# Layers 1 to 3 of a four-layer convolution kernel: sums, quantisation and layer 1 at other places in a round, zeros by VectorE

## The chip, the cores and the metric

The kernel runs on one core of one Trainium2 chip. The metric is device time in microseconds, lower is better. A core has five engines that each work through a queue of their own in order: TensorE (matmuls, PE), VectorE (DVE), ScalarE (ACT), GpSimd (POOL) and SyncE (SP). DMA transfers are issued here from the queues of GpSimd and SyncE.

## The reference, cut to what matters

Four convolution layers follow each other on 32 images of 8 channels and 256 x 256 pixels. Each layer normalises its input by groups of two channels and adds its output to its input.

```python
# layer 0: 15 steps of a coupled map, a small network and a gate
x = x + L0(_gn(x), ...)

# layer 1: 3x3 convolution, 8 channels to 8, on quantised values
sx = 127 / max|x|;  sw = 127 / max|weight|
qx = clip(round(x * sx), -127, 127);  qw = clip(round(weight * sw), -127, 127)
x = x + (conv(qx, qw) / (sx * sw) + bias)          # x inside is _gn(x)

# layer 2: 3x3 convolution, 8 channels to 8
x = x + (conv(_gn(x), weight) + bias)

# layer 3: 5x5 mean filter on each channel
x = x + depthwise_conv(_gn(x), weight)

def _gn(v, G=4, eps=1e-5):      # mean and variance over two channels and all pixels of an image
    return (v - mean) / sqrt(var + eps)
```

The maximum of |x| in layer 1 runs over all 32 images, so layer 1 cannot begin before layer 0 has finished with the last one.

## The kernel before, in words

Layer 0 fills the first five sixths of the span and is not touched. What follows is the second block of the kernel, which does layers 1, 2 and 3 for all images.

**Tiles.** For layers 1 and 2 an image lies in 128 partitions, 16 row classes times 8 channels, with 16 image rows of each class behind one another in a partition, 4096 values in all. The input of layer 1 is `qh` (bf16), that of layer 2 `xh` (fp32); both have one column of zeros at each side of a row. A convolution of a chunk of 512 outputs (`conv3`) is three matmuls on `qh` or `xh`, one for each horizontal shift, and a fourth on `qb` or `xb2`: 48 of their 72 rows hold the neighbour rows that lie in another partition. `beside` fills them with two DMAs of 24 rows from `qh` or `xh` on SP's queue. An image has 8 chunks (`NCH`). An fp32 matmul takes two passes of 0.43 us of TensorE, a bf16 matmul one of about 0.22. For layer 3 the partitions are 128 image rows, the tile `xr` has two halves (k) and 8 channels, and `xr2` holds the rows beyond the halves, filled by `beside3`.

**A round.** The loop over b runs through 35 rounds. In round b layer 3 works on image b-3, layer 2 on image b-1 and layer 1 on image b. A round has two halves, each run by `among(work, tasks)`: it takes up to eight steps of the generator `work` and after step i runs the tasks listed for i. The order in which these calls are made is the order in each engine's queue (`manual_schedule`); no scheduler reorders it.

- First half: the work is `layer3`, two steps for each group of two channels. After the first step (four matmuls of half 0), the second step has the four matmuls of half 1, the four halo and end matmuls, and two additions by VectorE (L831). The tasks are the sums of layers 1 and 2 of the last round, the normalisation of layer 2's input (`normal2`, L760) with the DMAs for `xb2`, the four quantisations of layer 1's input (`quantize1`: three VectorE operations of 1024 columns, L741, L703, L704, and one on ScalarE, L705) with the DMAs for `qb`, and `by_group`.
- Second half: the work is `both`, which alternates a chunk of layer 2 and a chunk of layer 1. The tasks are the four normalisations of layer 3's input (`normal3`, L792) and `beside3`. Layer 2 ends with 16 stores to DRAM on GpSimd's queue (L776), from where `load3` reads the image back as `y` in the layout of layer 3. Behind it GpSimd loads `x1`, the input of layer 1, a round ahead.

**Sums.** `stats_parts` is a generator in five parts: two `bn_aggr` at the round's end (L101, by `begin`), then a matmul over partitions and four small VectorE operations (L104 to L108), another matmul and an addition (L111, L112), a root on ScalarE (L115), and five small VectorE operations (L117 to L121). `by_group` turns layer 2's sums into scalars for layer 3: two VectorE operations (L131), a matmul (L133) and a copy (L135), all in one call.

**Order before.** In the first half, after step i: part i of both sums for i from 0 to 3, the one of layer 2 first; `normal2` after step 3; quantisation k after step k; `qb`'s DMAs after step 4; `by_group` after step 5. In the second half chunk i of layer 2 is followed by chunk i of layer 1. PSUM for the chunks is a pool of five buffers (`psv`), that for the sums one of three.

**Before the first round** the six tiles `qh`, `qb`, `xh`, `xb2`, `xr` and `xr2` are set to zero by GpSimd (L719), the scales of the quantisation are computed (`top`, L150 to L162, and L697 to L700), and the weights of layer 1 are quantised.

Of the kernel before, what the change touches and what calls it, by code (L numbers as in the profile page):

```python
# [22 lines left out]
HP, WP = H + 2, W + 2  # L23
# [37 lines left out]
def window(ap, offset, dims):  # L61

    return bass.AP(ap.tensor, ap.offset + offset, [list(d) for d in dims])
# [3 lines left out]
def kernel(  # L67
# [3 lines left out]
    nc = tc.nc  # L71
    B = x.shape[0]
# [54 lines left out]
    def by_group(psum, st):  # L127

        sel = small.tile([P, 4, 2], F32, name="sel")
        for j in range(2):  # L130
            nc.vector.tensor_scalar(sel[:, :, j], gsel_sb, st[:, j : j + 1], None, ALU.mult)  # L131
        ps = psum.tile([P, 512], F32, name="ps")
        nc.tensor.matmul(ps[:, 0:8], ones, sel.rearrange("p a b -> p (a b)"), start=True, stop=True)  # L133
        got = small.tile([P, 4, 2], F32, name="got")
        nc.vector.tensor_copy(got.rearrange("p a b -> p (a b)"), ps[:, 0:8])  # L135
        return got

    def beside(queue, t, src, q):


        row, long = HB * WP, (HB - 1) * WP - 2
        for i, (p, to, at) in enumerate(((P - C, 1, 0), (0, 0, 1))):
            queue.dma_start(
                t[q + 24 * i : q + 24 * i + 24, :, :].rearrange("p k w -> p (k w)")[
                    :, to * WP : to * WP + long
                ],
                window(src, p * row + at * WP, [[row, C], [1, 3], [1, long]]),
            )
# [19 lines left out]
    with ExitStack() as es:  # L168
# [6 lines left out]
        psum = es.enter_context(tc.tile_pool(name="ps_a", bufs=3, space=PSUM))  # L175
# [503 lines left out]
    with ExitStack() as es:  # L679
        wt = es.enter_context(tc.tile_pool(name="wt1", bufs=1))  # L680
        two = es.enter_context(tc.tile_pool(name="two", bufs=2))
        psum = es.enter_context(tc.tile_pool(name="ps_b", bufs=3, space=PSUM))
# [19 lines left out]
        def quantize(dst, t, s):  # L702
            nc.vector.tensor_scalar(t, t, s, MAX_Q, ALU.mult, ALU.min)  # L703
            nc.vector.tensor_scalar(t, t, -MAX_Q, ROUND, ALU.max, ALU.add)  # L704
            nc.scalar.activation(dst, t, AF.Copy, bias=-ROUND)  # L705
# [5 lines left out]
        qh = wt.tile([P, HB, WP], BF16, name="qh")  # L711
        qb = wt.tile([72, HB, WP], BF16, name="qb")
        xh = wt.tile([P, HB, WP], F32, name="xh")
        xb2 = wt.tile([72, HB, WP], F32, name="xb2")

        xr = wt.tile([P, 2, C, W + 4], F32, name="xr")
        xr2 = wt.tile([72, C, W + 4], F32, name="xr2")
        for t in (qh, qb, xh, xb2, xr, xr2):
            nc.gpsimd.memset(t, 0.0)  # L719

        def conv3(src, near, w, i):
            ps = ps_v.tile([P, 512], F32, name="psv")
            o = ps.rearrange("p (k w) -> p k w", w=W)
            for dx in range(3):
                nc.tensor.matmul(  # L725
                    o, w[:, dx, :], src[:, 2 * i : 2 * i + 2, dx : dx + W],
                    start=dx == 0, stop=False,
                )
            nc.tensor.matmul(  # L729
                o, w[0:72, 3, :], near[:, 2 * i : 2 * i + 2, 0:W], start=False, stop=True  # L730
            )
            return ps

        def load1(b):
            x1 = two.tile([P, NPX], F32, name="x1")
            nc.gpsimd.dma_start(x1, x1_d[b])
            return x1

        def quantize1(b, x1, k):
            t = two.tile([P, 1024], F32, name="tq")  # L740
            nc.vector.tensor_scalar(  # L741
                t, x1[:, bass.ts(k, 1024)], stat1[:, b, 0:1], stat1[:, b, 1:2],
                ALU.subtract, ALU.mult,
            )
            quantize(
                qh[:, 4 * k : 4 * k + 4, 1 : 1 + W],
                t.rearrange("p (r w) -> p r w", w=W), sc[:, 0:1],
            )

        def layer1(b, x1, x2, bn):  # L750
            for i in range(NCH):
                ps = conv3(qh, qb, w1_bf, i)
                c = x2[:, bass.ts(i, 512)]
                nc.scalar.activation(c, ps, AF.Identity, bias=b1_sb, scale=sc[:, 3:4])  # L754
                nc.vector.tensor_tensor(c, c, x1[:, bass.ts(i, 512)], ALU.add)
                nc.vector.bn_stats(bn[:, i, :], c)
                yield

        def normal2(x2, st):
            nc.vector.tensor_scalar(  # L760
                xh[:, :, 1 : 1 + W], x2.rearrange("p (k w) -> p k w", w=W),
                st[:, 0:1], st[:, 1:2], ALU.subtract, ALU.mult,
            )
            beside(nc.sync, xb2, xh, 0)

        def layer2(b, x2, bn):
            for i in range(NCH):
                ps = conv3(xh, xb2, w2_sb, i)
                c = x2[:, bass.ts(i, 512)]
                nc.vector.scalar_tensor_tensor(c, ps, b2_sb, c, ALU.add, ALU.add)  # L770
                nc.vector.bn_stats(bn[:, i, :], c)
                yield
            x3 = x3_d[b % 2]
            for r in range(RB):
                m = r % 4 * 4 + r // 4
                nc.gpsimd.dma_start(  # L776
                    window(x3, r * W, [[H * W, C], [RB * W, HB], [1, W]]),
                    x2[C * m : C * m + C, :].rearrange("p (k w) -> p k w", w=W),
                )
# [10 lines left out]
        def normal3(y, gs, g):  # L790
            for k in range(2):
                nc.vector.tensor_scalar(  # L792
                    xr[:, k, 2 * g : 2 * g + 2, 2 : 2 + W], y[:, k, 2 * g : 2 * g + 2, :],
                    gs[:, g, 0:1], gs[:, g, 1:2], ALU.subtract, ALU.mult,
                )
# [46 lines left out]
        x1s, x2s, ys, gss, sums = {}, {}, {}, {}, {}  # L842

        def among(work, tasks):
            for i in range(8):
                next(work, None)
                for task in tasks.get(i, ()):
                    task()
            for _ in work:
                pass  # L850

        def step(parts):
            return lambda: next(parts, None)
# [7 lines left out]
        with tc.manual_schedule():  # L861
            x1s[0] = load1(0)
            for b in range(B + 3):
                if b + 1 < B:
                    x1s[b + 1] = load1(b + 1)
                tasks = {i: [] for i in range(8)}
                if 2 <= b <= B + 1:
                    st3, parts3 = sums.pop(2)
                    for i in range(4):
                        tasks[i].append(step(parts3))  # L870

                    def groups():
                        gss[b - 2] = by_group(psum, st3)

                    tasks[5].append(groups)
                if 1 <= b <= B:
                    st, parts = sums.pop(1)
                    for i in range(4):
                        tasks[i].append(step(parts))
                    tasks[3].append(lambda: normal2(x2s[b - 1], st))  # L880
                if b < B:
                    for k in range(4):
                        tasks[k].append(lambda k=k: quantize1(b, x1s[b], k))
                    tasks[4].append(lambda: beside(nc.sync, qb, qh, 0))
                among(layer3(b - 3, ys.pop(b - 3)) if b >= 3 else iter(()), tasks)
                tasks = {}
                if 2 <= b <= B + 1:
                    for g in range(4):
                        tasks[g] = [lambda g=g: normal3(ys[b - 2], gss[b - 2], g)]
                    tasks[3].append(beside3)  # L890
                bns = [small.tile([P, NCH, 6], F32, name="bn") for _ in range(2)]
                if b < B:
                    x2s[b] = two.tile([P, NPX], F32, name="x2")
                ones_ = layer1(b, x1s[b], x2s[b], bns[0]) if b < B else iter(())

                def both():
                    for _ in layer2(b - 1, x2s[b - 1], bns[1]) if 1 <= b <= B else range(8):
                        next(ones_, None)
                        yield

                among(both(), tasks)
                if 1 <= b <= B:
                    sums[2] = begin(bns[1])
                    ys[b - 1] = load3(b - 1)
                if b < B:
                    sums[1] = begin(bns[0])
# [136 lines left out]
```

## Time and profile before

| | |
|---|---|
| median of 3 runs | 16326.91 us (16326.64 to 16338.44) |
| profiled execution | 16318.33 us, its span 16316.6 us |
| mean granted TensorE clock | 0.961 |
| TensorE busy over the span | 15452.2 us, 95% |
| VectorE / ScalarE / GpSimd busy | 72% / 35% / 34% |

| stretch of the span, us | what | TensorE busy | VectorE busy | granted clock | DMA share |
|---|---|---|---|---|---|
| 13592 to 13784.33 | zeros, scales, rounds 0 to 2 | 95.91 | 113.81 | 0.70 | 0.36 |
| 13784.33 to 16150 | rounds 3 to 31, with all three layers | 2227.35 | 1361.75 | 0.97 | 0.53 |
| 16150 to 16316.6 | rounds 32 to 34 | 149.63 | 45.74 | 0.97 | 0.43 |

Times inside the trace are counted from the start of the span. In the rows of the timeline the columns are start, busy time, engine, line of the code, operation, the tile written and the tiles read with their shapes, the number of instructions, and in brackets the idle time of the engine before the row with what ended it. "PE" is a matmul, "PEld" a load of weights, "SPq" a DMA issue on SP's queue. Digits are left out of tile names: `xb` is `xb2` and `x_d` is `x1_d` or `x3_d`. The chain of waits follows the work that ended last back from the end.

### The profile page before, as it was taken

To read this page: it belongs to the slowest core of one execution; us is meant where nothing else is said; L and a number is where in the kernel's file an instruction comes from. 1 tells how busy PE (TensorE), PEld (TensorE's weight loads), DVE (VectorE), ACT (ScalarE), POOL (GpSimd) and SP (SyncE) were. 2 spreads that over 40 slices of the span, in tenths; PEclk is the share of its full clock that TensorE was granted. 3 is DMA by queue.
4 is the path that set the end of the run, shared out by engine and by line. 5 is a ranking of instruction groups with operands and counts; after the bars stand their busy time and mean duration, and the time that the engine had idled before them with its cause. 6 is when DMAs were issued, how large, how long until landed. Compare 5 with 4: busy or idle time off the path is not lost.

```text
span 16316.6 us, 141125 instructions
## 1 busy us (share of the span) xinstructions
PE 15452.2 (95%) x42888; PEld 6215.7 (38%) x42888; DVE 11705.9 (72%) x14652; ACT 5726.7 (35%) x8862; POOL 5598.2 (34%) x9491
## 2 busy tenths in 40 slices
PE   6999999999999999999999999999999997999999
PEld 2333333333333333333333333333333332333333
DVE  7777777777777777777777777777777764555554
ACT  2433444443434434443434444343444442111110
POOL 1333333333333333333333333333333342111111
PEclk7999999999999999999999999999999998999999
DMA  4766666666666666666666666666666664555554
GB/s 104 148 146 144 150 147 144 147 150 146 149 144 148 150 147 147 144 147 145 147 142 149 148 144 147 141 148 146 147 149 147 146 134 98 119 119 119 119 118 105
DMA packets 1057742, 2276.12 MB, mean 139 GB/s; under 512 B 419740, under 2 KB 623508, under 8 KB 1050724
## 3 DMA queue, kind: packets, MB, share of 16 engines
q0 software_dynamic: 704512, 1492.80, 40.6%
q1 hardware_dynamic: 352484, 774.29, 23.4%
q8 instruction: 356, 5.83, 0.2%
q14 instruction: 390, 3.19, 0.1%
HBM read 1078.04 MB, written 471.38 MB: 95 GB/s over the span
## 4 chain that ended last, share of the span: by engine, by line
PE 74%; DVE 13%; DMA 7%; ACT 3%; issue 2%; SPq 1%; POOL 0%; DVEq 0%; ACTq 0%; POOLq 0%
PE ph L633 17%; PE psc L391 14%; PE psc L393 13%; PE pg L531 9%; DVE acc L338 7%; PE psv L725 5%; PE pn L610 5%; PE psv L811 4%; DMA qb<-qh 3%; DMA rings<-state 2%; PE psv L729 2%; PE pq L548 1%; PE pg L543 1%; PE pg L539 1%; DVE psc L402 1%
## 5 line engine op out<-in xcount | busy, mean ns | idle before, releaser
L338 DVE SCALAR_TENSOR_TENSOR acc<-strip,taps_sb,acc 128x1024 f32<-128x1024 f32 x3840 | 4930.4, 1284 | 124.8 <-DMA strip<-strip 4.7
L505 POOL DMA_DIRECT2D im<-xn_d x6144 | 3458.3, 566 | 3250.0 <-PE ph L633 1434.7
L633 PE MATMUL ph<-im,wp_sb 72*128 72x512 f32 x8192 | 4091.7, 615 | 308.8 <-ACT hh L638 251.3
L638 ACT ACTIVATE hh<-ph,bp_sb 128x512 f32<-128x512 f32 x4096 | 2755.8, 690 | 4441.9 <-PE ph L633 4385.7
L402 DVE SCALAR_TENSOR_TENSOR psc<-psc,flat 128x512 f32<-128x512 f32 x2880 | 1921.4, 696 | 2813.0 <-PE psc L393 2797.2
L391 PE MATMUL psc<-state,patch_sb 128*128 128x512 f32 x5760 | 2812.0, 626 | 74.1 <-ACT state L419 63.3
L393 PE MATMUL psc<-rings,ring_sb 80*128 80x512 f32 x5760 | 2713.5, 607 | 129.8 <-DMA rings<-state 129.8
L633 PEld LDWEIGHTS ph<-im,wp_sb 72*128 72x128 f32 x8192 | 1489.5, 193 | 2425.4 <-issue 1587.8
L419 ACT ACTIVATE state<-psc,minus 128x512 f32<-128x512 f32 x2688 | 1690.2, 690 | 1818.8 <-DVE psc L402 1713.1
L391 PEld LDWEIGHTS psc<-state,patch_sb 128*128 128x128 f32 x5760 | 1114.5, 199 | 1696.2 <-issue 1375.7
L393 PEld LDWEIGHTS psc<-rings,ring_sb 80*128 80x128 f32 x5760 | 1114.7, 194 | 1576.8 <-issue 1545.7
L569 POOL DMA_DIRECT2D x_d<-xc x256 | 146.9, 574 | 3493.1 <-DVE xc L564 3416.6
L811 PE MATMUL psv<-xr,w_sb 128*128 128x512 f32 x2560 | 1162.9, 600 | 1.3 <-DVE xr L792 1.3
L610 PE MATMUL pn<-hh,wu_sb 128*32 128x512 f32 x8192 | 1133.9, 609 | 3.3 <-ACT hh L638 3.3
L776 POOL DMA_DIRECT2D x_d<-x x512 | 321.0, 643 | 1941.0 <-DVE x L770 1696.3
L725 PE MATMUL psv<-xh,w_sb 128*128 128x512 f32 x1536 | 753.0, 629 | 9.6 <-issue 9.6
L531 PE MATMUL pg<-xq,wg_sb 128*128 128x512 f32 x1536 | 749.3, 626 | 0.0
L754 ACT ACTIVATE x<-psv,b_sb,sc 128x512 f32<-128x512 f32 x256 | 199.3, 779 | 1466.2 <-PE psv L729 1465.8
L531 PE MATMUL pg<-cq,wg_sb 128*128 128x512 f32 x1536 | 713.7, 601 | 0.0
L811 PEld LDWEIGHTS psv<-xr,w_sb 128*128 128x128 f32 x2560 | 466.1, 189 | 610.8 <-issue 606.0
L338 DVE SCALAR_TENSOR_TENSOR acc<-strip,taps_sb,d 128x1024 f32<-128x1024 f32 x480 | 613.2, 1277 | 0.0
L831 DVE TENSOR_TENSOR y<-psv,y 128x512 f32<-128x512 f32 x256 | 177.1, 692 | 593.7 <-PE psv L811 593.7
(163 smaller groups left out, 12188.9 us busy)
## 6 DMA issues: line engine op xcount, KB each, us to landing
im<-xn_d POOLq DMA_DIRECT2D x6144, 96.6 KB, 6.6
rings<-state SPq DMA_DIRECT2D x1920, 159.5 KB
rings<-state SPq DMA_DIRECT2D x1920, 106.3 KB
strip<-strip SPq DMA_DIRECT2D x960, 126.0 KB
xn_d<-xb POOLq DMA_DIRECT2D x128, 516.0 KB, 7.7
nr_d<-xb POOLq DMA_DIRECT2D x128, 516.0 KB, 7.2
xq<-nr_d POOLq DMA_DIRECT2D x128, 516.0 KB, 5.1
cq<-cr_d POOLq DMA_DIRECT2D x128, 516.0 KB, 7.9
```

Of the source, the lines that this page charges most:

```text
L338: nc.vector.scalar_tensor_tensor(acc, strip[:, dy : dy + RQ, dx : dx + W], taps_sb[:, 3 * dy + dx : 3 * dy + dx + 1], d2 if dy == 1 and dx ...
L391: nc.tensor.matmul(pss[-1], patch_sb[:, c, :], inner(c), start=True, stop=False)
L393: nc.tensor.matmul(pss[c % HALF], ring_sb[:, c, :], rings[half][:, c % HALF, 0 : TX * SY].rearrange("p (x y) -> p x y", y=SY)[:, :, 0:TY], ...
L402: nc.vector.scalar_tensor_tensor(ps, ps, FLOOR, dr[:, c], ALU.max, ALU.add)
L419: nc.scalar.activation(inner(c), pss[c % HALF], AF.Square, bias=minus)
L505: nc.gpsimd.dma_start(im[24 * dy : 24 * dy + 24, k, 0:run], window(xn_d[b % 3], at, [[HP * WP, C], [1, 3], [1, run]]),)
L531: nc.tensor.matmul(o, wg1_sb[:, s, dx, :], src[:, :, dx : dx + W], start=s == dx == 0, stop=False,)
L610: nc.tensor.matmul(pn[32 * q : 32 * q + 32, :], wu_sb[:, i, :], hh, start=i == 0, stop=i == 3,)
L633: nc.tensor.matmul(ph.rearrange("p (k w) -> p k w", w=W), wp_sb, im[:, :, j * WP : j * WP + W], start=True, stop=True,)
L638: nc.scalar.activation(hh, ph, AF.Relu, bias=bp_sb)
L725: nc.tensor.matmul(o, w[:, dx, :], src[:, 2 * i : 2 * i + 2, dx : dx + W], start=dx == 0, stop=False,)
L811: nc.tensor.matmul(pss[k].rearrange("p (c w) -> p c w", w=W), w3_sb[:, dx, :], xr[:, k, mine, dx : dx + W], start=dx == 0, stop=stop,)
```

## The change

The four quantisations, the parts of the two sums and the two sets of DMAs are listed for other steps of the first half. `by_group` becomes a generator of two parts. Layer 1 starts two chunks after layer 2 and does its last two chunks when layer 2 has ended. The order after each step of layer 3 becomes

| step | before | after |
|---|---|---|
| 0 | part 1 of both sums, quantisation 0 | part 1 of layer 1's sum, quantisation 0 |
| 1 | part 2 of both, quantisation 1 | parts 2 and 3 of layer 1's, part 1 of layer 2's |
| 2 | part 3 of both, quantisation 2 | part 4 of layer 1's, `normal2` with `xb2`'s DMAs, part 2 of layer 2's, quantisations 1 and 2 |
| 3 | part 4 of both, `normal2` with `xb2`'s DMAs, quantisation 3 | part 3 of layer 2's, quantisation 3, `qb`'s DMAs |
| 4 | `qb`'s DMAs | part 4 of layer 2's, first part of `by_group` |
| 5 | `by_group` | |
| 6 | | second part of `by_group` |

The zeros are set by VectorE, except for `xr2`; of `qh`, `xh` and `xr` only the border columns are set, since the rest is written before it is read. The neighbour tiles keep their 72 rows.

```diff
@@ by_group
             nc.vector.tensor_scalar(sel[:, :, j], gsel_sb, st[:, j : j + 1], None, ALU.mult)
+        yield None
         ps = psum.tile([P, 512], F32, name="ps")
...
-        return got
+        yield got
@@ zeros
-        for t in (qh, qb, xh, xb2, xr, xr2):
-            nc.gpsimd.memset(t, 0.0)
+
+        for t in (qh, xh):
+            for w in (0, WP - 1):
+                nc.vector.memset(t[:, :, w : w + 1], 0.0)
+        for t in (qb, xb2):
+            nc.vector.memset(t, 0.0)
+        for k in range(2):
+            for w in (0, W + 2):
+                nc.vector.memset(xr[:, k, :, w : w + 2], 0.0)
+        nc.gpsimd.memset(xr2, 0.0)
@@ first half of a round
+                if 1 <= b <= B:
+                    st, parts = sums.pop(1)
+                    for i in (0, 1, 1, 2):
+                        tasks[i].append(step(parts))
+                    tasks[2].append(lambda: normal2(x2s[b - 1], st))
                 if 2 <= b <= B + 1:
                     st3, parts3 = sums.pop(2)
                     for i in range(4):
-                        tasks[i].append(step(parts3))
+                        tasks[i + 1].append(step(parts3))
+                    parts4 = by_group(psum, st3)
+                    tasks[4].append(step(parts4))
 
                     def groups():
-                        gss[b - 2] = by_group(psum, st3)
-
-                    tasks[5].append(groups)
-                if 1 <= b <= B:
-                    st, parts = sums.pop(1)
-                    for i in range(4):
-                        tasks[i].append(step(parts))
-                    tasks[3].append(lambda: normal2(x2s[b - 1], st))
+                        gss[b - 2] = next(parts4)
+
+                    tasks[6].append(groups)
                 if b < B:
                     for k in range(4):
-                        tasks[k].append(lambda k=k: quantize1(b, x1s[b], k))
-                    tasks[4].append(lambda: beside(nc.sync, qb, qh, 0))
+                        tasks[(0, 2, 2, 3)[k]].append(lambda k=k: quantize1(b, x1s[b], k))
+                    tasks[3].append(lambda: beside(nc.sync, qb, qh, 0))
@@ second half of a round
                 def both():
-                    for _ in layer2(b - 1, x2s[b - 1], bns[1]) if 1 <= b <= B else range(8):
-                        next(ones_, None)
+                    twos = layer2(b - 1, x2s[b - 1], bns[1]) if 1 <= b <= B else iter(range(8))
+                    for i, _ in enumerate(twos):
+                        if i > 1:
+                            next(ones_, None)
                         yield
+                    for _ in ones_:
+                        pass
```

## The prediction

> **What bounds the kernel now.** The change touches only layers 1 to 3, so I cut the chain of waits at the point where layer 0 ends (13592) and read from there. It shows a fill up to 13784, then rounds of layer 3 followed by layers 2 and 1:
>
> ```profile
> 14032.27 3.44 PE psv L811 x8
> ...
> 14055.15 2.41 DVE xh L760
> 14061.41 1.20 SPq L143
> 14062.66 17.80 DMA qb<-qh
> 14081.12 3.75 PE psv L725 x6
> ...
> 14112.43 3.44 PE psv L811 x8
> ```
>
> Columns: start, length, what. The chain leaves TensorE in the middle of each round, for normalisation, a DMA issue and the transfer of `qb`. Rounds 3 to 31 (layer 3 starts at 13784.33 in round 3, 16150.00 in round 32) take 2365.67/29 = 81.57 us each. The view of waits over 13840 to 16140 (28 rounds) names what stops TensorE there:
>
> ```profile
> engine line waited for: us in total, times, longest us
> ...
> PE psv L729 <- DMA qb<-qh: 104.9, 28, 5.6
> ...
> PE ps L133 <- DVE sel L131: 29.4, 28, 1.1
> ```
>
> That is 3.75 and 1.05 us a round. The timeline shows that the first costs more than its idle time:
>
> ```profile
> 13992.52 0.81 PE L725 MATMUL psv<-qh,w_bf 128*128 128x512 bf16 x3
> 13998.72 0.61 PE L729 MATMUL psv<-qb,w_bf 72*128 72x512 bf16 x1 [5.38 <-DMA qb<-qh]
> 13999.12 5.33 PE L725 MATMUL psv<-xh,w_sb 128*128 128x512 f32 x6
> 14004.24 1.32 PE L729 MATMUL psv<-xb,w_sb 72*128 72x512 f32 x2
> 14005.40 0.81 PE L725 MATMUL psv<-qh,w_bf 128*128 128x512 bf16 x3
> 14006.05 0.38 PE L729 MATMUL psv<-qb,w_bf 72*128 72x512 bf16 x1
> 14006.27 2.74 PE L725 MATMUL psv<-xh,w_sb 128*128 128x512 f32 x6
> ```
>
> The same six passes take 5.33 us after the wait and 2.74 later: half the clock. I get the true loss by subtraction. The layer-3 half is 41.50 us (timeline, 14032.11 to 14073.61, the 1.05 included). A pair of chunks is 4.307 us (14006.43 to 14032.27 in the chain, six pairs), so eight are 34.46. 81.57 - 41.50 - 34.46 = 5.61 us lost per round: 3.7 idle, 1.9 slow clock.
>
> At the start, the timeline and the chain show one more stop:
>
> ```profile
> 13597.84 13.32 DVE L580 TENSOR_SCALAR ext<-ext,stat 128x2 f32<-128x2 f32 x1
> ...
> 13605.85 5.21 POOL xr L719 x2
> 13611.06 8.25 DMA x<-x_d
> 13619.34 0.82 DVE tq L741
> ```
>
> L580 takes 0.289 us at the median; here it ends as GpSimd's memsets end, and the load of x1 queues behind them too.
>
> **What the Trainium skill says.** "TensorE: Matmul & The Clock Gate", Part 1: an idle window of about 3.4 us halves the clock, about as much work restores it. The trace agrees: clock 1.00 before that wait, 0.50 over 13998 to 14004, 1.00 from 14007. "SBUF — State Buffer", Who interferes with whom: VectorE's two-port modes (tensor_scalar can enter them) and GpSimd lock each other out of a shared port pair for a whole instruction; L580's 13.32 us agrees. "DMA: Bandwidth & Descriptors", Issuing engines are not separate DMA queues: all transfers interleave on the same 16 engines; DMA share is 0.91 over 14062 to 14081, and the lone first `qb` transfer took 7.28 us against 17.80.
>
> **The change, part by part** (0 = layer 3's start in a round; numbers of the round at 14032).
>
> 1. Layer 1 two chunks late. Its first `qb` matmul now comes after three chunks of layer 2 instead of one. A layer-2 chunk is 8 passes of 0.43 = 3.44 us. Before: 41.5 + 3.44 + 0.65 = +45.6. After: 41.5 + 10.33 + 0.65 = +52.5.
>
> 2. Sums and quantisation. Today group 0's first L831 starts at +9.4 (14041.67); part 4 below adds 0.9. VectorE in the new order: two L831 to +11.9; L112 and four small operations of the other sum to 12.8; ACT's root runs beside them, no longer behind a quantisation; L117 to L121, 0.95, to 13.8; xh, 2.41, to 16.2. So `xb2` is issued at about +16.4 (today 14057.62, +25.4). Then two quantisations at 2.25 to +20.9. Group 1's L831, today at +19.6 (14051.88), could start at 20.5, so it is held 0.4, which costs nothing while PSUM buffers are free; its two to 22.5; the last quantisation 24.8; ACT 1.06. `qb` is issued at about +26 (today +29.1). At today's 17.8 us it lands near +45; the worst round today had it at +51.1 (13998.72 less 13947.59), which becomes about +48. Both are before +52.5. Wait and slow clock go: -5.61. If that cover failed, each late microsecond would return, with the clock loss.
>
> 3. `by_group` split. L131 moves to step 4, its matmul to step 6, more than a group later: -1.05 in rounds 3 to 33. Same instructions; nothing else is late.
>
> 4. New: the tail. Three layer-1 chunks now follow layer 2's last. Today the round's end reads
>
> ```profile
> 14111.60 0.75 DVE L770 SCALAR_TENSOR_TENSOR x<-psv,b_sb,x 128x512 f32<-128x512 f32 x1 [1.20 <-PE psv L729]
> 14112.47 0.78 ACT L754 ACTIVATE x<-psv,b_sb,sc 128x512 f32<-128x512 f32 x1 [3.53 <-PE psv L729]
> 14114.62 0.58 DVE L101 BATCH_NORM_AGGREGATE mv<-bn 128x2 f32<-128x48 f32 x2
> 14115.71 0.50 PE L104 MATMUL ps<-mv,gavr_sb 128*128 128x1 f32 x4
> ```
>
> With T = 14111.56 (last `xb2` matmul's end): VectorE has L770/L771 to T+1.5, layer 1 from T+1.72 (0.04 + ACT 0.78 + 0.9), three chunks at 1.33 (L755 and L756, as in round 0) to T+5.7, two L101 to T+6.3, L104's weights and slot to T+6.8. TensorE wants L104 at T+0.71+1.73+3.44 = T+5.9. New wait 0.9 us, in front of all layer-3 matmuls behind L104; bounds 0 (TensorE itself late) and 2.0 (1.4 us chunks plus a wait for ACT). I take 0.9, since each row shows its duration. Too short to lower the clock.
>
> 5. DMA order. SP's order stays `xb2`, `qb`, out, xr2, so nothing new is held behind a blocked issue. On POOL the 16 stores are issued before the last two layer-1 chunks, about 1.7 us earlier; `y` follows when they land. `xb2` (0.73 MB) now overlaps the stores instead of `y`. Today `y` is issued at +24 and lands at 22.3 median, +46. normal3 needs it at about +46.6; until +55 the five PSUM buffers let TensorE run on. Cost 0.
>
> 6. Fill. Rounds 1 and 2 have no layer 3 to hide `xb2`. Round 1: L117 at 13659.40 now follows one quantisation (13655.0), ACT's 1.06 and the root, 13656.4: -3.0. Round 2: 13725.03 to about 22.0, with the other sum's five operations and four earlier ones out of the way: -4.4, plus 0.9 for the tail. Sum -6.5 (bounds -3, -9).
>
> 7. Memsets. GpSimd keeps xr2 (1.8, half of xr), so x1 is issued near 13594.5 and lands at 13603; L580 ends near 13598; the 5.1 us from there to the quantised weights end at 13603. VectorE adds `qb`, `xb2` and eight borders. It has rows for 128 columns (0.165 us) and one (0.059): 0.83 ns a column, 3.5 us for 4128. "VectorE: DVE Perf Modes", Zero memsets can be issued as uint32, says a cycle per element and half as many for bf16: an estimate of 4.3 and 2.15. With 0.8 for borders, 6.1 to 9.4. First quantisation between 13603 (memsets hidden in the chain's gaps) and 13612.5 (in series) against 13619.34; I take 13610: -9.3, ends -16 and -6.8.
>
> **Sum.** Rounds 3 to 31: 29 x (-5.61 - 1.05 + 0.9) = -167.0. Rounds 32 and 33: -2.1 + 0.9. Fill -6.5, start -9.3. Total -184.0. The profiled execution took 16318.33 (span 16316.6 and 1.7 around it), so 16134; the median of the runs, 16326.91, lies 8.6 above it: 16143.
>
> **Rivals.**
> A. `qb` still late. For: 17.8 us is mostly contention, and `y` and x1 (3 MB) are in flight with it. Against: `xb2` is out of its way, and 6 us of slack. If it takes 28 us it lands at +55, 2.4 late: 29 x 2.4 = 70, 16213. Chance 0.14 (16185 to 16294).
> B. No change. L104's stall reaches the clock's limit: 4 idle and 2.2 slow clock against 6.66 saved; with fill and start 16300. For: TensorE stands in order behind it. Against: three more microseconds of VectorE work than I count. 0.05.
> C. Slower. `y` is late: `xb2` runs into the stores, they land late, POOL holds `y`, normal3 blocks VectorE's queue, and PSUM fills. From +55 each microsecond stops TensorE, beyond 3.4 with 2.5 of slow clock. It outweighs the gain from `y` landing at about +59; at +61 it costs 8.5 a round, 29 x 8.5 = 247, 16390. For: POOL's waits for stores are 208 us already and SP's rows use few partitions. Against: that is 15 us later than today, and `y` then has fewer rivals. 0.11.
>
> **Numbers.** Forecast 0.70, own range 16105 to 16185 (tail 0 to 2.0: -27, +32; start and fill, -10, +6). A 0.14, B 0.05, C 0.11. The range 16115 to 16240 keeps nearly all of the forecast and most of A. Within 0.2% (33 us, about what a measurement here can tell): 0.05; slower 0.11; faster 0.84.
>
> **What would show it.** Right: no TensorE wait for `qb`, no half clock in rounds 3 to 31, no wait at L133, a wait of about 1 us at L104, rounds of 75.8 us, `xb2` issued 16 us into a round, first L741 near 13610. Wrong: VectorE idle before L792 for `y`, TensorE waiting at L725 for PSUM, or L831 held behind the quantisations.

## The result, and the profile after

| | before | after |
|---|---|---|
| median | 16326.77 us (4 runs) | 16153.82 us (16148.80 to 16156.96, 4 runs) |
| ratio | | 0.9893, 95% interval 0.9880 to 0.9906 |
| span of the profiled execution | 16316.6 us | 16155.1 us |

The kernel is 1.07% faster. The forecast was 16143; the result is 10.9 us above it and inside its range.

The totals also carry layer 0, which was not changed and still differs from run to run: its last gate matmul ended at 13588.9 in the profile before, at 13594.6 after, and between 13542.6 and 13613.1 in all runs below. So parts of the change are measured inside the stage. Three lengths are used throughout, read from the timeline of TensorE: the mean length of rounds 3 to 31, from the first layer-3 matmul of one round to that of the next, and its two halves, divided where layer 2 begins. For the span they add up: 5.6 us later at the end of layer 0, -12.6 up to round 3, -152.2 in rounds 3 to 31, -2.3 behind them, together -161.5 of -161.5.

| | round, mean (shortest to longest) | first half | second half | end of layer 0 to round 3 |
|---|---|---|---|---|
| before | 81.57 (78.60 to 84.64) | 41.50 | 40.07 | 195.2 |
| after | 76.33 (76.32 to 76.33) | 40.74 | 35.59 | 182.7 |

All rounds after have the same length to 0.01 us: TensorE waits for no transfer in them any more. The view of windows of the changed kernel over rounds 3 to 31 (start and end, length, then busy time and count of TensorE, its weight loads, VectorE, ScalarE and GpSimd, the granted clock, the DMA share and GB/s) has the clock at 1.00, where it was 0.97:

```profile
13777.22:15990.69 2213.47, 2179.96 (x5859) 913.96 (x5858) 1342.42 (x2495) 311.79 (x407) 406.70 (x551) 1.00 0.60 126
```

The view of waits of the changed kernel, over 13840 to 16000, answers to the one shown before. `qb` and L133 are gone as causes of TensorE's waits; in their place stand two short ones, and the first line shows GpSimd holding `y` for far longer than before:

```profile
POOL y L794 <- DMA x_d<-x: 517.2, 27, 22.0
...
DVE xr L801 <- DMA y<-x_d: 56.4, 31, 4.1
...
PE psv L734 <- ACT x L763: 24.3, 28, 0.9
...
PE ps L104 <- DVE mv L101: 8.3, 29, 0.3
```

The second of TensorE's waits is the tail that was forecast. The timeline of a round's end shows it: three layer-1 chunks run through ScalarE and VectorE behind layer 2's last one, and the sums (L101) end just too late for L104.

```profile
14003.80 0.75 DVE L779 SCALAR_TENSOR_TENSOR x<-psv,b_sb,x 128x512 f32<-128x512 f32 x1 [1.20 <-PE psv L738]
14004.66 2.52 ACT L763 ACTIVATE x<-psv,b_sb,sc 128x512 f32<-128x512 f32 x3 [3.53 <-PE psv L738]
14009.45 0.58 DVE L101 BATCH_NORM_AGGREGATE mv<-bn 128x2 f32<-128x48 f32 x2
14010.09 0.38 PE L104 MATMUL ps<-mv,gavr_sb 128*128 128x1 f32 x2 [0.29 <-DVE mv L101]
```

The first was not forecast. In each round the matmuls of one layer-2 chunk wait for ScalarE to read the layer-1 chunk that TensorE finished just before:

```profile
13990.19 0.38 PE L738 MATMUL psv<-qb,w_bf 72*128 72x512 bf16 x1
13990.61 0.78 ACT L763 ACTIVATE x<-psv,b_sb,sc 128x512 f32<-128x512 f32 x1 [3.53 <-PE psv L738]
13991.44 1.13 PE L734 MATMUL psv<-xh,w_sb 128*128 128x512 f32 x2 [0.87 <-ACT x L763]
```

These two chunks don't depend on each other; only a common PSUM buffer can join them. In the program as built, that layer-2 chunk (the sixth) does have the bank of the layer-1 chunk issued right ahead of it, 30 times; in the kernel before no chunk takes over the bank of the chunk right ahead of it. (A bank is what one of the five buffers occupies.)

The transfers moved too. The DMA issues of one round before (layer 3 starts at 14112.27), from the timeline of SP and of GpSimd:

```profile
14137.81 1.42 SPq L143 DMA_DIRECT2D xb<-xh  x2
14141.38 6.83 SPq L143 DMA_DIRECT2D qb<-qh  x2
...
14138.25 2.44 POOL L785 DMA_DIRECT2D y<-x_d  x2 [8.34 <-issue]
14140.68 0.56 POOL L736 DMA_DIRECT2D x<-x_d  x1
```

and of one round after (start 14082.53):

```profile
14098.05 1.43 SPq L144 DMA_DIRECT2D xb<-xh  x2
14107.82 4.91 SPq L144 DMA_DIRECT2D qb<-qh  x2
...
14121.36 1.84 POOL L794 DMA_DIRECT2D y<-x_d  x2 [21.65 <-issue]
14123.19 0.56 POOL L745 DMA_DIRECT2D x<-x_d  x1
```

Counted from the start of the round: `xb2` went from +25.5 to +15.5, `qb` from +29.1 to +25.3, and `y` with x1 from +26 to +39. Before, 4 MB of loads (two of 1 MB for `y`, 2 MB for x1) were issued in the 3 us ahead of `qb`; after, they are issued 13 us behind it. In rounds 3 to 31 the first load of `y` left between +23.6 and +27.7 before (median +25.2), and between +30.3 and +39.2 after (median +38.2).

At the start, the timeline of the changed kernel has VectorE's memsets in the middle of the last sums, and the load of x1 waiting for layer 0's store instead of for memsets:

```profile
13601.07 1.78 DVE L724 MEMSET qb<- 72x2064 uint32 x1 [0.38 <-issue]
13603.67 3.50 DVE L724 MEMSET xb<- 72x4128 f32 x1 [0.81 <-issue]
13603.68 1.07 POOL L745 DMA_DIRECT2D x<-x_d  x2 [4.44 <-DMA x_d<-xc]
...
13613.58 0.29 DVE L581 TENSOR_SCALAR ext<-ext,stat 128x2 f32<-128x2 f32 x1
```

VectorE's scaling of the extremes, L580 before and L581 here, takes 0.29 us instead of 13.32. `qb`'s first DMAs leave 32.4 us after the end of layer 0 instead of 40.6.

### The profile page after: what moved, and what is told of

It is laid out like the page before. It is cut to its first block, busy times and chain, and to the rows that moved or that the text cites. A ratio compares the mean times of both kernels' runs of the same rounds, so it can differ in the third digit from the quotient of the medians.

```text
span 16155.1 us, 141092 instructions
## 1 busy us (share of the span) xinstructions
PE 15414.4 (95%) x42888; PEld 6200.3 (38%) x42888; DVE 11677.2 (72%) x14662; ACT 5724.0 (35%) x8862; POOL 5611.6 (35%) x9486
## 5 line engine op out<-in xcount | busy, mean ns | idle before, releaser
L785 POOL DMA_DIRECT2D x_d<-x x512 | 370.5, 740 | 1387.0 <-DVE x L779 1161.0
L734 PE MATMUL psv<-xh,w_sb 128*128 128x512 f32 x1536 | 714.8, 601 | 32.4 <-ACT x L763 26.1
L414 DVE SCALAR_TENSOR_TENSOR strip<-acc 128x1024 f32<-128x1024 f32 x448 | 549.8, 1227 | 15.3
```

The costliest lines, as they stand in the source:

```text
L734: nc.tensor.matmul(o, w[:, dx, :], src[:, 2 * i : 2 * i + 2, dx : dx + W], start=dx == 0, stop=False,)
```

## The experiments

Twelve runs follow, two of them repeats. Four parts of the change can be separated: the order in the first half, the split of `by_group`, the delay of layer 1, and the zeros. A ratio compares a kernel with executions of the kernel before made beside it, whose median lay between 16292.37 and 16321.93 us. Kernels without a ratio were executed once, and only their traces are read. Where `qb` is late, rounds also differ from one execution to the next: 81.57 us in the kernel before, 80.97 with the zeros alone changed.

**The delay of layer 1 alone.**

```diff
 # before
-    for _ in layer2(...) ...:           # cut; twos is this same generator
-        next(ones_, None)
+    for i, _ in enumerate(twos):
+        if i > 1:
+            next(ones_, None)
         yield
+    for _ in ones_:
+        pass
```

> The kernel before with one part of the change: layer 1 two chunks behind layer 2. Theory (the wait for qb was lost because its first use came too early): qb lands at +48 of a round (worst seen +51), its first use moves from +45.6 to +52.5, so the wait and the half clock go (-5.61 us a round), and the two costs seen in the changed kernel come with it: 1.13 at the chunk that takes over the PSUM buffer just used, 0.29 at L104. The wait at L133, 1.05, stays. Round 81.57 - 5.61 + 1.13 + 0.29 = 77.4 us, 29 rounds give -121, about 16205. Rival (the earlier issue of xb2 and qb in the changed kernel did it): qb still late in most rounds, rounds above 79 us, 16250 or more.

Measured: rounds 77.50 us, first half 41.83, second half 35.67; median 16176.60, ratio 0.9928 (0.9911 to 0.9945). The view of waits has

```profile
PE ps L133 <- DVE sel L131: 29.5, 28, 1.1
PE psv L725 <- ACT x L754: 24.3, 28, 0.9
```

and no line for `qb`. The delay is enough to hide the transfer, and both of its costs come with it, 1.2 us in the second half and 0.33 in the first.

**The order alone.**

```diff
 # after
-        yield None                      # by_group in one call again
...
-    tasks[6].append(groups)
+    tasks[5].append(groups)
...
-        if i > 1:                       # layer 1 beside layer 2 again
-            next(ones_, None)
+        next(ones_, None)
...
-        ...                             # the memsets of the change
+        for t in (qh, qb, xh, xb2, xr, xr2):
+            nc.gpsimd.memset(t, 0.0)
```

> The kernel before with the changed order of sums, normal2, quantisations and DMAs in the first half, by_group still in one call (at step 5), layer 1 not delayed, zeros by GpSimd. Theory: qb is issued at about +25.5 and lands near +45, its first use is at +45.6, so the wait shrinks from 3.7 to 0 to 1 us and never reaches the length at which the clock is halved; L133's 1.05 stays. Rounds of 76 to 77 us, 16317 - 29 x 5 = about 16170. Rival (the transfers are limited by what else is in flight, and an earlier issue does not make them land earlier): qb lands at +48 as before, wait 2.5 us or more, rounds of 79 us or more, 16240 or more. If this and the delay alone each take most of the wait away, the two parts are not worth their sum.

Measured: rounds 75.96 us with a spread of 0.01, halves 41.50 and 34.45; median 16119.32, ratio 0.9897 (0.9877 to 0.9918). The only wait of TensorE on a VectorE result or a transfer in the rounds is

```profile
PE ps L133 <- DVE sel L131: 29.5, 28, 1.1
```

The order alone takes away the whole 5.61 us of wait and slow clock (81.57 - 75.96), with nothing left for the delay to hide.

**The split of `by_group` alone.**

```diff
 # before
+        yield None                      # in by_group, ahead of the matmul
...
+    parts4 = by_group(psum, st3)
+    tasks[4].append(step(parts4))
...
-    tasks[5].append(groups)
+    tasks[6].append(groups)
```

> The kernel before with by_group in two parts (steps 4 and 6) and nothing else. Theory: the wait at L133 goes (-1.05 a round), but TensorE then only waits longer for qb, whose landing does not depend on L133: rounds stay within 0.5 us of 81.57, time within 15 us of before. Rival (the two waits add): -1.05 a round, -33 in all, 16294.

Measured: first half 40.18 instead of 41.50, second half 42.38 instead of 40.07, rounds 82.56; median of 20 runs 16322.76, ratio 1.0021 (1.0013 to 1.0029). The wait moved to

```profile
PE psv L730 <- DMA qb<-qh: 133.5, 26, 6.3
```

5.1 us a round. The theory holds in kind: while `qb` is late, a shorter first half only makes TensorE wait longer. It comes out a little slower than the kernel before beside it (16292.37, 23 runs). In the timeline of TensorE the first `qb` matmul comes at +50.0 of a round on average, against +49.5 before, so nothing of the 1.3 us gained in the first half is left; what follows it takes 32.5 us against 32.1, at a mean granted clock over the rounds of 0.96 against 0.97. Part of this can be the difference between executions; why `qb` lands later at all is not shown.

**The PSUM buffers in turn**, added to the changed kernel.

```diff
+        banks = [ps_v.tile([P, 512], F32, name=f"psv{i}", bufs=1) for i in range(5)]
+        turn = [0]
+        def bank():
+            turn[0] += 1
+            return banks[turn[0] % 5]
...
-            ps = ps_v.tile([P, 512], F32, name="psv")
+            ps = bank()                 # in conv3, and the same in layer3
```

> The changed kernel with the five PSUM buffers of the chunks taken in turn, instead of from the pool, which hands one layer-2 chunk the buffer that the layer-1 chunk just ahead of it uses. Theory: the second half's loss of 1.13 us a round is that buffer alone: second half 34.46 instead of 35.59, rounds of 75.2, 29 x 1.13 = 33 us less than the changed kernel, about 16121. Rival (TensorE waits because ScalarE or VectorE are behind): the wait moves to another chunk, rounds stay at 76.3.

Measured: second half 34.45, rounds 75.19; median 16098.98, ratio to the kernel before 0.9877 (0.9861 to 0.9894). The wait did not move elsewhere. The 1.13 us were the bank.

**One chunk of delay instead of two**, with the buffers in turn: `if i > 1` becomes `if i > 0`.

> The changed kernel with the PSUM buffers in turn and layer 1 one chunk behind layer 2 instead of two. Theory: with two layer-1 chunks after the last of layer 2 VectorE ends the sums one chunk (1.33 us) sooner and TensorE only 0.87 sooner, so the 0.29 at L104 goes; qb has until +48. Rounds of 74.9 us. If L104's wait had another cause than the length of this tail it stays at 0.29: 75.2.

Measured: rounds 74.77, first half 40.30 instead of 40.74. L104 waited once in the whole window. The tail's length sets that wait.

**The delay undone in the changed kernel.**

```diff
 # after
-    for i, _ in enumerate(twos):
-        if i > 1:
-            next(ones_, None)
+    for _ in twos:
+        next(ones_, None)
         yield
-    for _ in ones_:
-        pass
```

> The changed kernel with the delay of layer 1 undone: chunk i of layer 1 again follows chunk i of layer 2; order, split by_group and zeros stay. Theory (the order alone brings qb in time, and the delay only brings its own costs): the PSUM wait of 1.13 and the one of 0.29 at L104 go, qb is needed at +44.5 and is there. First half 40.45, second half 34.45, rounds of 74.9 us, 29 x 1.42 = 41 us less than the changed kernel. Rival (with L133's 1.05 gone TensorE comes too early for qb, and the delay is what covers it): a wait for qb of 0.5 to 2 us comes back, rounds of 75.5 to 77 us.

Measured: rounds 74.64 us, halves 40.19 and 34.45; median 16100.13, ratio 0.9869 (0.9839 to 0.9900). No wait for `qb`: the rival falls.

**When does `qb` land?** In the kernel with the order alone, layer 1's chunk was put ahead of layer 2's, so that TensorE asks for `qb` at +42.2.

```diff
 # order alone
-    ...                                 # layer 2's chunk first
+    for _ in range(8):
+        next(ones_, None)
+        next(twos)
+        yield
+    for _ in twos:
+        pass
```

> A probe of when qb lands: the kernel with the changed order alone, with chunk i of layer 1 ahead of chunk i of layer 2, so that qb is needed at about +42.2 of a round instead of +45.6. If a transfer of qb still takes 17.8 us from its issue near +25.5, as the prediction took it, it lands near +44 to +45 and TensorE waits 2 to 3 us for it in each round, rounds of 78 to 79 us. If the transfer is shorter once xb2 and the loads of y and x1 no longer run beside it, qb is there before +42 and TensorE does not wait for it; rounds then stay near 76 us but for PSUM.

Measured: rounds 75.95, no wait for `qb` in 28 rounds, although it was issued at +24.7. So it lands less than 17.5 us after its issue in every round. In the chain before it landed 19.1 us after it (14061.41 to 14080.46; the 17.8 leaves out the issue), so that duration does not carry over.

**A late `qb` with an early `xb2`.**

```diff
 # order alone
-    tasks[(0, 2, 2, 3)[k]].append(lambda k=k: quantize1(b, x1s[b], k))
-    tasks[3].append(lambda: beside(nc.sync, qb, qh, 0))
+    tasks[(0, 2, 2, 5)[k]].append(lambda k=k: quantize1(b, x1s[b], k))
+    tasks[5].append(lambda: beside(nc.sync, qb, qh, 0))
```

> The kernel with the changed order alone, but the last quantisation and qb's DMAs put off to step 5: qb is issued near +35.7 of a round, later than the +29.1 of the kernel before, while xb2 stays early (+15.5). Theory (qb is in time not because it is issued 3 us earlier but because xb2 is out of its way and, by slowing the stores, holds the loads of y and x1 back behind it): the transfer takes about 9 us, as the first one of the kernel does with nothing beside it, and lands at about +45 against a need at +45.6: a wait of 0 to 2 us, rounds of 76 to 78 us. Rival (the transfer always takes its 17.8 us, and the earlier issue decided): it lands at +53, a wait of 7 us and half the clock behind it, rounds of 84 us or more.

Measured: rounds 77.40 on average, from 75.95 to 83.55. `qb` left at +35.4 or a little later and was in time in half of the rounds (27.6 us of waits in 14 of 28), so there it took less than about 10 us. When `y` leaves tells the rounds apart. In five of the 29 it left 3.3 us or more ahead of `qb`, and exactly in these TensorE waited long, 3.2 to 4.4 us; in the others, where it left at most 2.7 us ahead or behind, the wait was 1.8 us or less. The longest round starts at 15628.08:

```profile
15660.04 1.23 POOL L786 DMA_DIRECT2D y<-x_d  x1 [13.90 <-DMA x_d<-x]
15664.06 1.40 SPq L143 DMA_DIRECT2D qb<-qh  x2
15678.20 0.61 PE L730 MATMUL psv<-qb,w_bf 72*128 72x512 bf16 x1 [4.37 <-DMA qb<-qh]
15678.60 5.33 PE L726 MATMUL psv<-xh,w_sb 128*128 128x512 f32 x6
```

The same rounds give the price of a wait. Those of 0.2 to 1.8 us made a round longer than 75.95 by their own length and at most 0.2 us more; those of 3.2 to 4.4 us cost 1.6 to 3.2 us on top, with the six passes behind taking 5.33 us again.

**The loads behind `qb`.** The kernel before, but SP issues `y` and x1, and after `qb`.

```diff
 # before
     tasks[4].append(lambda: beside(nc.sync, qb, qh, 0))
+    tasks[4].append(lambda: ys.update({b - 2: load3(b - 2)}))
+    tasks[4].append(lambda: x1s.update({b + 1: load1(b + 1, nc.sync)}))
...
-    x1s[b + 1] = load1(b + 1)           # at the start of a round
-    ys[b - 1] = load3(b - 1)            # at its end
...
-                nc.gpsimd.dma_start(             # in load3; load1 takes the queue
+                nc.sync.dma_start(
```

> The kernel before with the loads of y and x1 issued by SP behind qb's DMAs instead of by GpSimd; order, by_group, layer 1 and zeros as before. xb2 still at +25.4 and qb at +29.1. Theory (3 MB of y and x1 beside qb make it late): qb shares the engines with xb2 alone and lands before +45.6; the wait and the half clock go, rounds of 76 us. Rival (the early xb2 and the earlier issue are what counts): a wait of 2 us or more stays, rounds of 79 us or more.

Measured: rounds 76.02 us. The timeline of SP, in a round that starts at 14097.52:

```profile
14123.04 1.43 SPq L143 DMA_DIRECT2D xb<-xh  x2
14126.39 7.61 SPq L143 DMA_DIRECT2D qb<-qh  x2
14134.36 6.86 SPq L785 DMA_DIRECT2D y<-x_d  x2
14141.27 3.05 SPq L736 DMA_DIRECT2D x<-x_d  x1
```

`xb2` at +25.5 and `qb` at +28.9 are where they were before; `y` moved from +26 to +36.8. With that the wait is gone (8.6 us in all before weight loads, none before a matmul). The edit moves the loads to another queue as well as to a later time. But with the order alone they stayed on GpSimd's queue, left behind `qb` too, and `qb` was in time; and in the run above, on that queue too, the wait went with the lead of `y`. So what made `qb` late was the company of `y` and x1, not its own time of issue.

**The zeros alone.**

```diff
 # before
-        for t in (qh, qb, xh, xb2, xr, xr2):
-            nc.gpsimd.memset(t, 0.0)
+        ...                                  # the memsets of the change
```

> The kernel before with the zeros set by VectorE (xr2 by GpSimd) and nothing else. Theory: only the stretch from layer 0's last matmul to the first layer 3 gets shorter, 195.2 to about 187 us, since x1 is loaded earlier and VectorE is not held at L580; rounds stay at 81.6 on average; about 8 us in all, which the time of one run can't tell from nothing. Rival (VectorE's memsets stand in front of the scales): no gain in that stretch.

Measured: `qb`'s first DMAs leave 32.8 us after layer 0 instead of 40.6, and `xb2`'s in round 1 are 7.9 us earlier too, but round 3 starts only 3.5 us earlier (191.7). This is one execution, and the same stretch differs by 3.6 us between the two profiles of the changed kernel, so what is left of this gain at round 3 is not settled.

**The changed kernel and its version without the delay, again, beside each other.**

> The changed kernel again, on the same chip as the next one, to compare the two: ratio to the kernel before about 0.989, rounds of 76.33 us.

> The changed kernel without the delay of layer 1, again beside the changed kernel: rounds of 74.64 us instead of 76.33, 29 x 1.69 = 49 us, and about 4 us in the first rounds: ratio to the changed kernel about 0.9967.

Measured: rounds of 76.33 and 74.64 us again; medians 16134.06, ratio 0.9886 (0.9866 to 0.9907), and 16087.36, ratio 0.9866 (0.9844 to 0.9887). The medians lie 46.7 us apart. The intervals of the ratios overlap, since layer 0 moves the totals; the rounds, which have no spread, decide. The version without the delay beats both the kernel before and the changed one.

## Why the prediction was right, and where its steps were off

The sum was right because the largest term was: the wait for `qb` and the slow clock behind it went away whole. The total came closer than its parts. From the end of layer 0 on, the profiles differ by 167.1 us where 184.0 were forecast, 16.9 us short; that the medians miss by only 10.9 is luck, for the end of layer 0 moves by tens of microseconds between executions of one kernel (13594.6 and 13568.5 in the two profiles of the changed one).

- **What bounded the rounds.** Right. The 5.61 us got by subtraction is what the order alone gives back, 5.61; the idle time of 3.75 us would have missed a third of it, the half clock.
- **Part 2, order.** The conclusion holds, the term that carried it was mis-sized. The issue times came out (+15.5 and +25.3 against +16.4 and +26). But "at today's 17.8 us it lands near +45" took the transfer's duration as fixed while the change moved what runs beside it: it lands less than 17.5 us after its issue instead of 19.1, so the slack was larger than forecast. In rival A, the 3 MB of `y` and x1 are 4.
- **Part 1, the delay.** Sufficient, and not needed: the order alone reaches 75.96. It was counted as cover; the runs show it as cost.
- **Part 4, the tail.** Right in mechanism. First half 40.74 less 40.19 without the delay: 0.55 us against 0.9. The sums end where it put them, 6.3 us behind layer 2's last matmul (14003.76 to 14010.03). But it charged 0.5 us for L104's weights and slot, while layer 3 goes on after 0.30 (at 14010.33), and 0.14 of that slot is spent without the delay too.
- **Part 5, transfers.** The cost of 0 was right, the reason not. It took `y`'s issue (+24) and its 22.3 us as they were before the change. In the changed kernel `y` leaves at +38 in the median but then takes 8.6 us, so it lands at +46.6 instead of +48.4. The stores ahead of it land later, and they overlap with `xb2`, which now leaves at +15.5; with `qb` put off as well (`qb_late`) `y` still leaves at +34.8, so `qb` is not the main cause. No run moved `xb2` alone, so that it is what holds the stores back is argued, not shown. Rival C's mechanism did happen, up to its last link: VectorE waited 56.4 us for `y` in all, and PSUM covered it.
- **What was missed.** The PSUM wait of 1.13 us a round. The prediction has no term for it; it counted on the five buffers being free. It had named TensorE waiting for PSUM, and VectorE idle for `y`, as signs of being wrong: both appeared, the first from a shared bank and not from a late `y`, the second without a cost.
- **Part 3, the split.** 1.05 was forecast, 1.31 is what the first half shows (41.50 to 40.19), provided `qb` is not late; alone it gains nothing.
- **Rounds 3 to 31, sum.** Forecast -5.61 - 1.05 + 0.9 = -5.76, measured -5.61 - 1.31 + 0.55 + 1.13 = -5.24. The difference makes 15 us over 29 rounds.
- **Parts 6 and 7, fill.** Forecast -15.8, measured -12.6. The memsets cost VectorE a little less than forecast (1.78 and 3.50 us and 0.4 for the borders, 5.7 in all against 6.1 to 9.4), and they stood in the chain as assumed: L111 waited 6.9 us for the last of them. The load of x1 waited 4.4 us for a store of layer 0, which was not counted. Apart, the order shortened the stretch to round 3 by 7.0 us (188.2 in `order_only`; forecast 7.4 without the tail's 0.9), the zeros by 3.5 (forecast 9.3), each in one execution. So as far as these show it, the gain put down to the memsets was the term that was too large.

Rival A and rival B did not occur.

## What to carry to other kernels

A transfer's duration read from a profile belongs to its neighbours in time: before moving its issue forward or its use back, look at which bulk loads were issued just ahead of it, and try putting those behind it. Price a long wait on TensorE from the length of the period, not from the idle column: here the matmuls behind waits of 3 us and more ran at half clock, those behind waits below 2 us did not. A buffer pool with as many buffers as seem needed may still hand out the one in use, so look for a consumer of the *previous* chunk as what ended the wait. Price a wait removed upstream of a longer one at nothing.

## What was not expected of the hardware

- Loads of 1 MB (`y`, two per round) took 22.3 us from issue to landing at the median when `xb2` and `qb` were in flight with them, and 8.6 us when these had gone ahead; x1's 2 MB went from 28.0 to 14.0 us.
- When two transfers of 24 rows each (`xb2`, 0.73 MB) were issued 10 us earlier, among the last of the 16 stores, the load of `y` that waits for these left 10 us (`qb_late`) to 13 us (the changed kernel) later in the median, though the mean DMA share of the rounds is only 0.6.
- VectorE's memset of a bf16 tile of 4128 columns is recorded as 2064 columns of uint32 and takes 1.78 us, the fp32 tile of 4128 columns 3.50 us: about 0.85 ns a recorded column.
